# Where the pieces of a tile's second stage stand between the sums of the next tile: 1, 2, 2, 2, 2 in place of 2, 2, 2, 2, 1

## The chip, the core and the metric

The kernel runs on one core of a Trainium2 chip. TensorE (PE) multiplies, VectorE (DVE) and ScalarE (ACT) do the elementwise work, GpSimd (POOL) issues the gathers, SyncE (SP) the other transfers. The metric is the device time of one execution, in microseconds (us). The median of three runs before the change is 1955.56 us (1948.99 to 1957.19).

## What is computed

Two graph attention layers over 3327 nodes with 1024 features, each with a residual and a layer norm. The adjacency matrix is sparse (a few per mille of the entries, plus the diagonal). The change touches only the second layer, which has one head:

```python
h = input @ W
f1 = h @ a1
f2 = h @ a2
e = jax.nn.leaky_relu(f1 + f2.T, negative_slope=ALPHA)
scores = jnp.where(adj > 0, e, neg)
attention = jax.nn.softmax(scores, axis=1)
h_prime = attention @ h
return jax.nn.relu(h_prime)
...
x = _layernorm(x + _L1_gnn_ref(x, adj, L1_gnn_W, L1_gnn_a1, L1_gnn_a2), axis=-1)
```

Since attention @ (input @ W) is (attention @ input) @ W, the kernel first takes the weighted mean of the neighbours' input rows, and multiplies that mean by W afterwards.

## The kernel before

The nodes are 26 tiles of 128 targets. A first stage projects layer 0 and makes lists of neighbours; then layer 0 and layer 1 run one after the other through the same function, `pipeline`, and the change is in the call for layer 1 (L1083). A tile's edges are gathered in five steps: four blocks of four groups (32 targets each, 128 slots per group), and one "end" block for what did not fit.

For layer 1 (class `Target`) a tile t goes through these functions. `prepare` (L946) transposes a score column into the T bank on PE (L949), takes its exponential on ScalarE (L951) and makes one-hot marks on VectorE (L819, L823). `fetch` (L968) issues the gathers of one block on POOL (L803). `weights` (L974) makes a block's weights `es` by three operations on VectorE (L981, L982, L984). `sums` (L987) multiplies weights by gathered rows into three A banks (L993); for the four blocks it works in groups of 32 rows of the array, for the end block on all 128. `close` (L998) divides: the mean goes to `z` (L1001 to L1010, ScalarE and VectorE).

`finish` (L1015) is a generator of ten pieces. Pieces 1 and 2 (`transposed`, L176 and L179) transpose half of the mean each, four 128x128 blocks into one bank with the tag T, and ScalarE copies the bank to `xT`. Pieces 3 to 6 are the product of the mean with the first 512 columns of W (L1025), two matmuls to a piece, in a bank with the tag S; piece 6 ends with L1028, where VectorE takes the maximum with zero, adds the residual and so frees the bank. Pieces 7 to 10 do the same for the other 512 columns; piece 10 also queues `settle` (L1033), the layer norm (L192 to L199, with a square root on ScalarE, L195, that loads its own table) and the store.

In the profile one f32 matmul of L1025 or L993 leaves two records, so two pieces of the product are eight records.

Nothing is reordered by a scheduler here: the part runs under a manual schedule, and each engine executes in the order in which the program is written. That order comes from `pipeline`: at each step b of tile t it emits weights for the next step, the sums of this step, the gathers for the next tile, and then as many pieces of the waiting `finish` of the tile before as `behind[b]` says; `late` pieces are run at the beginning of a tile, ahead of its first sums. With late = 1 and a placeholder put in front at tile 1 (L1072), piece 10 of a `finish` is left to the beginning of the tile after. The eight PSUM banks are shared out by tag (L744): five A, one S, one T, and one E for `way`, where the weights are worked out. The core of the loop:

```python
for b in range(EB + 1):
    if b == 0 and t:
        tiles[t - 1].close()
        run(work, late)
    ...
    tg.sums(b)
    if t + 1 < NT:
        tiles[t + 1].fetch(b)
    run(work, behind[b])
    if t or b:
        run(ahead)
```

Of the kernel before, what the change touches and what calls it, by code (L numbers as in the profile page):

```python
# [26 lines left out]
def kernel(  # L27
# [715 lines left out]
    def sparse(own):  # L743
# [43 lines left out]
        def run(work, steps=1):  # L787

            while work and steps:
                try:  # L790
                    next(work[0])
                    steps -= 1
                except StopIteration:
                    work.popleft()
# [243 lines left out]
        def pipeline(kind, late, behind, get):  # L1038

            tiles = [kind(t) for t in range(NT)]
            work = deque()
            get(0)
            tiles[0].prepare()
            for b in range(EB + 1):
                tiles[0].fetch(b)
            tiles[0].weights(0)
            for t, tg in enumerate(tiles):  # L1050
                tg.begin()
# [4 lines that stand above are left out]
                    if b == 0 and t + 1 < NT:  # L1056
                        get(t + 1)
                    if b == 2 and t + 1 < NT:
                        tiles[t + 1].prepare()
                    if b == 0:  # L1060
                        tg.own()
                    if b < EB:
                        tg.weights(b + 1)
                    elif t + 1 < NT:
                        tiles[t + 1].weights(0)
# [6 lines that stand above are left out]
                if t == 0 and late:  # L1072
                    work.append(iter(range(1)))
                work.append(tg.finish())
            tiles[-1].close()
            run(work, late)
            run(ahead, -1)
            run(work, -1)
            run(ahead, -1)

        with tc.manual_schedule():
            pipeline(Layer0, 0, (1, 1, 1, 1, 1), get_edges)
            pipeline(Target, 1, (2, 2, 2, 2, 1), lambda t: None)  # L1083


    def by_pairs(own):
# [119 lines left out]
    with arm.Else():  # L1206
        with ExitStack() as own:
            sparse(own)
# [23 lines left out]
```

## Time and profile before

The profile is of one execution with a span of 1901.5 us. Rows below are sums over stretches of it (us of busy time, and what part of the stretch that is):

| stretch | what runs | PE | DVE | ACT | POOL | DMA GB/s |
|---|---|---|---|---|---|---|
| 0 to 450 us | projection, lists | 420.85 (94%) | 384.24 | 224.77 | 119.78 | 108 |
| 450 to 1200 us | layer 0 for the most part | 444.23 (59%) | 467.28 | 176.90 | 470.14 | 361 |
| 1210 to 1895 us | layer 1 | 653.32 (95%) | 292.51 | 144.70 | 432.51 | 356 |

In layer 1 the costliest groups are L1025 (383.3 us busy, 604 ns a record), L993 over gathered blocks (206.2 us, 464 ns a record, four of them side by side), and the gathers of L803 (415.7 us on POOL, 999 ns each). A row of the timeline has the start, the duration, the engine, the line, the operation, output and input, and how often; in brackets is the idle time of the engine ahead of it and what ended it. PEld is PE's weight load, which goes ahead of its matmul. A row of the list of waits has who waited for whom, the total in us, how often, and the longest.

### The profile page before, as it was taken

The page shows a single profiled execution, that of the slowest core. Times are in us where ns is not written, and L with a number is a line of the kernel's source. Part 1 is how long each engine was busy: PE and PEld are TensorE (multiplying, and loading weights), DVE is VectorE, ACT ScalarE, POOL GpSimd, SP SyncE. Part 2 cuts the span into 40 slices and gives each one's busy share as a digit, 9 for nine tenths or more (in the row PEclk, how much of TensorE's full clock was granted, in tenths as well). Part 3 has the DMA queues.
Part 4 walks back from the last instruction along what each step waited for, and adds up shares of the span by engine and source line. Part 5 has one row for each costly group of instructions (what it writes and reads, how often), then busy time and mean ns, then how long its engine had stood idle before and what let it go on. Part 6 is the DMA issues. An engine that isn't in the chain of part 4 may idle for free.

```text
span 1901.5 us, 38079 instructions
## 1 busy us (share of the span) xinstructions
PE 1518.5 (80%) x14663; PEld 902.4 (47%) x14663; DVE 1146.6 (60%) x3058; ACT 546.6 (29%) x1422; POOL 1030.2 (54%) x1391
## 2 busy tenths in 40 slices
PE   8799999999266555656556565399999999999997
PEld 5465556666255554545545454144444444444443
DVE  6699999986386665666666666244444444444442
ACT  5544455542022222222222222012222212222220
POOL 4322222220576666676676764677766667666650
PEclk9899999999678777787788877699999999999999
DMA  7656455411899999999999997899999999999980
GB/s 184 101 133 131 100 99 99 88 62 39 325 373 404 396 392 394 366 405 392 386 392 389 394 376 273 332 398 410 400 372 382 380 378 369 359 371 373 366 326 33
DMA packets 171068, 567.76 MB, mean 299 GB/s; under 512 B 27690, under 2 KB 34346, under 8 KB 170878
## 3 DMA queue, kind: packets, MB, share of 16 engines
q0 software_dynamic: 131056, 455.68, 67.6%
q1 hardware_dynamic: 39822, 109.56, 15.4%
q8 instruction: 118, 1.93, 0.4%
q14 instruction: 72, 0.59, 0.1%
HBM read 578.85 MB, written 42.97 MB: 327 GB/s over the span
## 4 chain that ended last, share of the span: by engine, by line
PE 52%; DMA 24%; DVE 12%; ACT 6%; issue 4%; POOL 2%; SPq 0%; DVEq 0%; ACTq 0%; POOLq 0%
DMA src<-h_d,idx 20%; PE mm L1025 20%; PE acc L993 12%; PE mm L479 12%; DVE e L870 3%; PE acc L898 3%; ACT junk L311 3%; PE tr L176 2%; POOL src L803 2%; DMA src<-y_d,idx 2%; DVE pr L931 1%; PE acc L882 1%; DMA wt<-in_L_gnn_W_dram 1%; ACT xT L179 1%; PE xp L411 1%
## 5 line engine op out<-in xcount | busy, mean ns | idle before, releaser
L803 POOL DMA_INDIRECT src<-h_d,idx x416 | 441.1, 1060 | 209.1 <-PE acc L898 58.0
L803 POOL DMA_INDIRECT src<-y_d,idx x416 | 415.7, 999 | 221.6 <-PE acc L993 96.3
L898 PE MATMUL acc<-src,e 128*32 128x128 f32 x6656 | 278.5, 337 | 253.6 <-DVE e L870 253.5
L479 PE MATMUL mm<-wt,xT 128*128 128x347 f32 (+1 forms) x1248 | 402.3, 469 | 3.3 <-DMA wt<-in_L_gnn_W_dram 2.9
L1025 PE MATMUL mm<-wt,xT 128*128 128x512 f32 x832 | 383.3, 604 | 0.8 <-DVE o L1028 0.8
L898 PEld LDWEIGHTS acc<-src,e 128*32 128x32 f32 x6656 | 234.8, 137 | 311.3 <-DVE e L870 284.3
L479 PEld LDWEIGHTS mm<-wt,xT 128*128 128x128 f32 x1248 | 228.3, 192 | 106.0 <-issue 4.2
L1025 PEld LDWEIGHTS mm<-wt,xT 128*128 128x128 f32 x832 | 152.2, 190 | 199.5 <-issue 179.1
L993 PE MATMUL acc<-src,es 128*32 128x342 f32 (+1 forms) x2496 | 206.2, 464 | 33.8 <-DVE es L984 31.0
L870 DVE TENSOR_TENSOR e<-oh,way 128x1024 f32<-128x1024 f32 x130 | 158.7, 1221 | 63.2 <-ACT w L868 62.8
L993 PEld LDWEIGHTS acc<-src,es 128*32 128x32 f32 x2496 | 71.6, 111 | 158.6 <-issue 112.9
L868 ACT ACTIVATE w<-way 128x32 f32<-128x32 f32 (+1 forms) x130 | 24.6, 189 | 407.7 <-DVE way L866 395.6
L1028 DVE SCALAR_TENSOR_TENSOR o<-mm,y 128x512 f32<-128x512 f32 x52 | 35.9, 691 | 166.2 <-PE mm L1025 166.2
L1007 ACT ACTIVATE z<-y,ri 128x342 f32<-128x342 f32 (+1 forms) x78 | 39.5, 570 | 313.9 <-DVE ri L1003 313.9
L865 DVE TENSOR_TENSOR way<-src,re 128x32 f32<-128x32 f32 x104 | 20.8, 200 | 175.1 <-DMA src<-h_d,idx 157.6
L179 ACT ACTIVATE xT<-tr 128x512 f32<-128x512 f32 x104 | 59.4, 596 | 151.0 <-PE tr L176 150.9
L981 DVE TENSOR_TENSOR way<-way,src 128x128 f32<-128x128 f32 x104 | 31.1, 299 | 90.0 <-ACT way L951 44.2
L850 ACT ACTIVATE own<-own,es 128x128 f32<-128x128 f32 x208 | 63.6, 388 | 57.4 <-DVE es L847 57.4
L311 ACT ACTIVATE junk<-ad 128x3328 uint8<-128x3328 uint8 x26 | 78.4, 3014 | 2.5 <-POOL ad L308 2.5
L882 PE MATMUL acc<-end,e 128*128 128x128 f32 x416 | 67.7, 328 | 13.3 <-DVE e L870 13.3
L296 POOL CAST mvs<-r 128x8 bf16<-128x8 f32 x26 | 6.0, 232 | 122.8 <-ACT r L295 122.8
L335 POOL TENSOR_TENSOR place_of<-cnt 128x1 f32<-128x1 f32 x26 | 4.9, 190 | 121.0 <-ACT cnt L328 101.5
(188 smaller groups left out, 1959.7 us busy)
## 6 DMA issues: line engine op xcount, KB each, us to landing
h_d<-ht SPq DMA_DIRECT2D x26, 520.0 KB
own<-h_d SPq DMA_DIRECT2D x26, 520.0 KB
y_d<-y SPq DMA_DIRECT2D x26, 514.0 KB
y<-y_d SPq DMA_DIRECT2D x26, 514.0 KB
x<-in_x_dram SPq DMA_DIRECT2D x25, 512.0 KB
y<-in_x_dram SPq DMA_DIRECT2D x25, 512.0 KB
out_dram<-o SPq DMA_DIRECT2D x25, 512.0 KB
ad<-in_adj_dram POOLq DMA_DIRECT2D x25, 415.9 KB
```

Source lines behind the costliest of these rows:

```text
L176: nc.tensor.transpose(tr[:, k, :], src[:, (4 * g + k) * P : (4 * g + k + 1) * P], ident)
L179: nc.scalar.activation(part, tr, AF.Copy)
L311: nc.scalar.activation(junk, ad, AF.Copy, accum_out=self.deg)
L479: nc.tensor.matmul(acc, xT[t][:, k, :], wt[:, k, CUTS0[c] : CUTS0[c + 1]], start=k == 0, stop=k == KT - 1)
L803: nc.gpsimd.indirect_dma_start(out=s[:, g, :w], out_offset=None, in_=table[:, :], in_offset=bass.IndirectOffsetOnAxis(ap=idx[:, t, b * NG ...
L850: nc.scalar.activation(hn, hn, AF.Copy, scale=es[:, n : n + 1])
L870: nc.vector.tensor_tensor(e, oh.unsqueeze(2).to_broadcast([P, ng, H, wide]), wp.unsqueeze(3).to_broadcast([P, ng, H, wide]), OP.mult,)
L882: nc.tensor.matmul(self.acc[h // 4][:, h % 4, :], e[:, 0, h, :], rowsof[:, 0, h, :], start=False, stop=h % 4 == 3,)
L898: nc.tensor.matmul(self.acc[h // 4][g * GT : (g + 1) * GT, h % 4, :], e[:, g, h, :], rowsof[:, g, h, :], start=first and h % 4 == 0, stop= ...
L993: nc.tensor.matmul(self.acc[c][to, :m], es[:, g, :], s[:, g, CUTS[c] : CUTS[c + 1]], start=b == 0, stop=b == EB,)
L1007: nc.scalar.activation(z[:, cut], self.res[:, cut], AF.Copy, scale=ri[:, 1:2])
L1025: nc.tensor.matmul(acc, xT[:, k, :], wt1[:, k, half], start=k == 0, stop=k == KT - 1)
```

## The change

One tuple: how many pieces of the waiting `finish` follow each of a tile's five sums in layer 1.

```diff
         with tc.manual_schedule():
             pipeline(Layer0, 0, (1, 1, 1, 1, 1), get_edges)
-            pipeline(Target, 1, (2, 2, 2, 2, 1), lambda t: None)
+            pipeline(Target, 1, (1, 2, 2, 2, 2), lambda t: None)
```

The number of pieces in a tile is the same. Both halves of transposes use the one T bank, so the second half can't begin before ScalarE has emptied the bank of the first. With the change the sums of the second step stand between the two halves. All later pieces move by one: the pieces after sums 0 to 4 were 1-2, 3-4, 5-6, 7-8 and 9, and are 1, 2-3, 4-5, 6-7 and 8-9. Piece 10 stays at the beginning of the tile after. On VectorE, L1028 of the first product moves behind the weights of the end block; on ScalarE, the square root of the layer norm comes to stand between the two copies to `xT`.

## Prediction

> **What bounds the kernel now.** I read the page first (engine shares, slices), then the busy time by windows inside layer 1, then the list of waits there, then the timeline of one tile, and last the timeline of the drain after the last tile, because a wait that the change creates already occurs there once. Layer 1 runs from about 1210 us to the end. The table by windows (columns: busy time and number of instructions of PE, PE's weight loads, DVE, ACT, POOL; clock; DMA share; GB/s) says who limits it; each window here is one tile, 26 us:
>
> ```profile
> 1485.00:1511.00 26.00, 25.31 (x146) 10.93 (x145) 11.45 (x34) 5.84 (x10) 17.44 (x18) 1.00 1.00 371
> 1511.00:1537.00 26.00, 25.31 (x146) 11.02 (x145) 11.75 (x36) 5.84 (x10) 17.31 (x18) 1.00 0.98 370
> ```
>
> PE is busy 25.31 of 26.00 us, at the full clock; DVE, ACT and POOL are far from full. So PE sets the pace, and the idle 0.69 us per tile is all that a reordering can take away directly. The waits between 1230 and 1880 us (total us, times, longest) name it:
>
> ```profile
> POOL src L803 <- PE acc L993: 96.0, 119, 3.7
> ...
> DVE way L981 <- DMA src<-y_d,idx: 17.6, 7, 4.2
> ...
> PE tr L176 <- ACT xT L179: 20.0, 26, 2.8
> ```
>
> The third line is the idle: the second group of transposes waits for ScalarE to empty the one T bank. Leaving out the longest (the drain), (20.0 - 2.8) / 25 = 0.69 us a tile. The gathers wait for PE to free source buffers (first line), and VectorE waited for gathered rows 7 times only, so DMA, though 98 to 100% busy by share, does not set the end here. In the timeline of one tile (start, duration) the wait looks like this:
>
> ```profile
> 1515.40 1.93 PE L993 MATMUL acc<-src,es 128*32 128x341 f32 x24
> ...
> 1517.26 0.43 PEld L176 LDWEIGHTS tr<-ident,z 128*128 128x128 f32 x4 [0.56 <-DVE way L982]
> ...
> 1517.96 0.60 ACT L179 ACTIVATE xT<-tr 128x512 f32<-128x512 f32 x1 [4.84 <-PE tr L176]
> 1518.61 0.42 PEld L176 LDWEIGHTS tr<-ident,z 128*128 128x128 f32 x4 [0.92 <-ACT xT L179]
> ...
> 1519.19 0.16 PEld L993 LDWEIGHTS acc<-src,es 128*32 128x32 f32 x8 [0.17 <-DVE sg L194]
> ...
> 1540.94 1.93 PE L993 MATMUL acc<-src,es 128*32 128x341 f32 x24
> ```
>
> From one tile's first sums to the next is 1540.94 - 1515.40 = 25.54 us. The first transposes hold PE from 1517.26 to 1518.61 (1.35 us, with the wait), the second from 1518.61 to 1519.19 (0.58 us, without one).
>
> The drain has the other wait. Here all ten pieces of the last tile stand in a row, so piece 7 follows piece 6 with nothing between, and both use the one S bank:
>
> ```profile
> 1876.15 0.42 PEld L176 LDWEIGHTS tr<-ident,z 128*128 128x128 f32 x4 [2.99 <-ACT xT L179]
> 1876.54 0.30 PEld L1025 LDWEIGHTS mm<-wt,xT 128*128 128x128 f32 x2
> ...
> 1884.36 0.19 PEld L1025 LDWEIGHTS mm<-wt,xT 128*128 128x128 f32 x1 [0.24 <-issue]
> 1886.16 0.30 PEld L1025 LDWEIGHTS mm<-wt,xT 128*128 128x128 f32 x2 [1.61 <-DVE o L1028]
> 1886.69 0.19 PEld L1025 LDWEIGHTS mm<-wt,xT 128*128 128x128 f32 x1 [0.24 <-issue]
> ```
>
> VectorE's own rows put that L1028 at 1885.41, for 0.69 us; the weight load follows 0.06 us after its end.
>
> [...] L1028 held VectorE 4.17 us in this tile while it waited for PE. [...] a weight load of L1025 after the 32-row sums comes 0.56 us after the last one, between products 0.24 us. [...] the trace's waits of 0.7 to 0.8 us are followed by loads at the usual 0.43 us, and only after the drain's 2.99 us do four come 0.85 us apart, so no clock is lost in the loop.
>
> **The change, part by part.** No instruction is added or removed, and the queues of POOL and SP stay the same. [...] It concerns the 25 finishes inside the loop; the last runs in the drain, which is the same.
>
> *The T wait goes.* Before, transposes cost 1.35 + 0.58 = 1.93 us a tile. After, half 1 is followed by sums 1, as half 2 was: 0.58 us. Half 2 then stands before a product in the same tiling mode: the drain shows 1876.54 - 1876.15 = 0.39 us for that. Gain 1.93 - 0.58 - 0.39 = 0.96 us; from below it is bounded by the idle 0.69 us. The copy of half 1 (0.60) lies beside sums 1 (1.87 us), that of half 2 beside piece 3 (four records at 0.43 = 1.72 us).
>
> *An S wait comes.* Pieces 6 and 7 now stand side by side, where sums 3 stood between them and hid L1028. Piece 7 waits until L1028 has emptied the bank. Price from the drain: from the last load before it to the third after its return 1886.69 - 1884.36 = 2.33 us, where three steps of 0.43 = 1.29 would do: 1.04 us. From below, PE's idle row there, 0.79; from above, the plain gap in loads, 1.80 - 0.43 = 1.37. I take 1.04, as the third load has both the restart and its catching up in it. Queued behind the waiting matmul are piece 7, sums 4, and then 8, 9, 10: all of PE. Nothing else fills it.
>
> *VectorE's order.* L1028 moves behind the three operations of weights(4) (3 x 0.30 us plus gaps, about 0.95). They need the end rows, gathered some 24 us before, and stood behind L1028 only by order; they now run before piece 6 ends, so L1028 is ready when PE is. Behind L1028 stand weights(0) of the next tile (0.95 us), whose sums come after sums 4 and three pieces, so over 7 us later. Cost nothing.
>
> *ScalarE's order.* The square root with its table load (1.28 + 0.20 us) now stands between the two xT copies. Counted from the sums 0 at 1515.40, with the durations of the same timeline: copy 1 ends at 3.2, the root's input is there at 3.7, the root ends at 4.7, or 5.2 if the table came late; half 2's transposes end near 5.0. Copy 2 then ends by 5.8, and L949, which needs the T bank, is due at 4.31 + 0.39 + 1.72 = 6.4. Hidden, with 0.6 us to spare.
>
> *Room elsewhere.* close() gets three pieces instead of two to hide under, but it ended 1.7 us early already: worth nothing. Sums 1 comes at 2.44 and its es was ready at 2.09 (1517.20 + 0.29): no wait, though close.
>
> Sum: (1.04 - 0.96) x 25 = +2.0 us, 1955.56 + 2.0 = 1957.6 us. With the bounds crossed: (0.79 - 0.96) x 25 = -4, (1.37 - 0.96) x 25 = +10, and (1.37 - 0.69) x 25 = +17.
>
> **The rivals.** *The exchange is about even* (above): 1957.6. *The T wait goes and the S wait is mostly hidden*: at the most 0.96 x 25 = 24, so 1932; half hidden, 1944. For it: L1028 might find PE with slack elsewhere. Against it: PE is 97% busy and its order is fixed, and the drain shows the S wait whole. *The S wait is larger*: at 1.37 and a gain of 0.69, 1973; if weights(4) held L1028 up by 0.95 us, (0.08 + 0.95) x 25 = +26, 1981. [...] Against it: VectorE idled over 4 us at L1028, which is more than weights(4) takes. *A wait at L949* behind root and table load: a microsecond a tile, +25, 1981; against it the 0.6 us to spare.
>
> **How the numbers follow.** Even exchange 0.70; T gain without its price 0.11; larger S wait 0.13; L949 0.06. Within 0.5% is 9.8 us, so faster 0.11, same 0.70, slower 0.19. The runs before spread 8 us of themselves. The range takes in the even exchange with its bounds and that spread, half of the faster rival and the start of the slower ones: 1945 to 1972.
>
> **What would show it.** Right: the wait of L176 on xT falls from 20 us to the drain's 2.8; a wait of L1025 on L1028 appears 25 more times at 0.8 us idle; the tile period is 25.6 us. Wrong: L1028 starting later than 0.1 us after piece 6 ends, a wait of L949 on xT, of sums 1 on es, or a new wait for gathered rows; or a period of 24.7, if the S wait were hidden.

## The result, and the profile after

| | median us | lowest to highest | executions |
|---|---|---|---|
| before | 1956.38 | 1948.99 to 1958.43 | 4 |
| after | 2022.80 | 2019.75 to 2023.61 | 4 |

The ratio is 1.0326, with a 95% interval of 1.0301 to 1.0352: slower by 66 us. The prediction was 1957.6, in a range that ended at 1972. It was wrong, and no rival reached this time either.

The profile after spans 2017.7 us. The list of waits of PE in the middle of layer 1, 1310 to 1930 us, has the same columns as the one shown of before (total us, times, longest). A line that ends in "issue" is an idle time for which this trace holds no releasing event; the timeline below shows what such a line stands for.

```profile
PE tr L949 <- issue: 20.8, 18, 1.9
PE mm L1025 <- issue: 20.6, 13, 2.2
PE mm L1025 <- DVE o L1028: 20.6, 9, 6.5
PE tr L949 <- ACT xT L179: 4.2, 3, 1.9
```

The wait of L176 on `xT` is gone, as foretold. The wait of piece 7 on L1028 has come, but with 41.2 us (20.6 + 20.6, in 22 places) it is 1.87 us on the mean, not 0.79. And L949, which was to be hidden with 0.6 us to spare, waits 21 times, 25.0 us in all.

One tile of the timeline after (start, duration, engine, line, operation, output and input, how often, idle time ahead and what ended it):

```profile
1632.29 0.66 PE L176 MATMUL tr<-ident,z 128*128 128x128 f32 x4
1632.98 0.60 ACT L179 ACTIVATE xT<-tr 128x512 f32<-128x512 f32 x1 [6.56 <-PE tr L176]
...
1634.74 0.66 PE L176 MATMUL tr<-ident,z 128*128 128x128 f32 x4
1634.89 0.20 ACT L195 ACTIVATE sg<-sg 128x1 f32<-128x1 f32 x1
...
1635.23 1.88 PE L1025 MATMUL mm<-wt,xT 128*128 128x512 f32 x4
...
1637.64 0.60 ACT L179 ACTIVATE xT<-tr 128x512 f32<-128x512 f32 x1 [2.55 <-PE mm L1025]
...
1638.30 0.32 PE L949 MATMUL tr<-ident,sd 128*128 128x128 f32 x1 [1.18 <-issue]
...
1645.90 1.98 PE L1025 MATMUL mm<-wt,xT 128*128 128x512 f32 x4
...
1648.69 0.69 DVE L1028 SCALAR_TENSOR_TENSOR o<-mm,y 128x512 f32<-128x512 f32 x1 [6.76 <-PE mm L1025]
...
1649.44 1.99 PE L1025 MATMUL mm<-wt,xT 128*128 128x512 f32 x4 [1.55 <-DVE o L1028]
```

Copy 1 starts 0.03 us after half 1 ends (1632.29 + 0.66 = 1632.95). Half 2 ends at 1635.40, ScalarE is free since 1635.09 (the root, L195), and nothing but PE is left to wait for: yet copy 2 starts at 1637.64, 2.24 us late. The trace has an event of PE's semaphore at 1637.62, just before that start, so by this trace it is the signal that comes late, and not ScalarE that answers it late. L949 needs the bank that copy 2 empties, and so comes 1.18 us after piece 3. The same at piece 6: it ends at 1647.88, VectorE has been idle for 6.76 us, and L1028 starts at 1648.69, 0.81 us late (the event before it is at 1648.67); piece 7 then idles 1.55 us.

The table by windows has the same tile (columns as before: busy time and number of PE, PE's loads, DVE, ACT, POOL; clock; DMA share; GB/s):

```profile
1632.29:1660.09 27.80, 25.07 (x147) 10.56 (x143) 11.37 (x34) 5.84 (x10) 16.94 (x17) 1.00 0.92 341
```

The tile takes 27.80 us at full clock; 25.62 was predicted. Three tiles in the middle of this profile take 31.6 to 34.5 us, and some at the beginning of layer 1 take longer than steady ones too. In one of the three L1028 is so late that piece 7 waits 6.51 us, and its four records then take 3.78 us instead of 1.98 (the second row, again from the timeline after). In another tile a wait of 2.06 us is followed by four records in 2.83 us (the first row):

```profile
1469.14 2.83 PE L1025 MATMUL mm<-wt,xT 128*128 128x512 f32 x4 [2.06 <-issue]
1529.89 3.78 PE L1025 MATMUL mm<-wt,xT 128*128 128x512 f32 x4 [6.51 <-DVE o L1028]
```

The granted clock is 0.50 from 1470.2 to 1473.5 us, after the wait of 2.06 us, and 0.50 from 1530 to 1535, after the one of 6.51. Another wait of 2.10 us in the same profile (it ends at 1297.89) was followed by four records in the usual 1.98, so the length of a wait doesn't tell it by itself. So such a wait can be paid for twice.

### The profile page after: what moved, and what is told of

It reads as the page before. It is cut to its first block, busy times and chain, and to the rows that moved or that the text cites. A ratio compares the mean times of both kernels' runs of the same rounds, so it can differ in the third digit from the quotient of the medians.

```text
span 2017.7 us, 38080 instructions
## 1 busy us (share of the span) xinstructions
PE 1673.8 (83%) x14663; PEld 936.4 (46%) x14663; DVE 1142.0 (57%) x3058; ACT 546.1 (27%) x1422; POOL 1029.3 (51%) x1391
## 4 chain that ended last, share of the span: by engine, by line
PE 71%; issue 12%; DVE 6%; ACT 5%; DMA 3%; another core or an unknown queue 2%; POOL 1%; SPq 0%; POOLq 0%; DVEq 0%; ACTq 0%
PE mm L1025 19%; PE acc L898 17%; PE acc L993 12%; PE mm L479 11%; PE acc L882 5%; PE acc L890 3%; ACT junk L311 3%; PE tr L176 2%; DMA src<-h_d,idx 1%; DMA wt<-in_L_gnn_W_dram 1%; PE den L907 1%; PE xp L411 1%; DVE top L274 1%; DMA src<-y_d,idx 1%
## 5 line engine op out<-in xcount | busy, mean ns | idle before, releaser
L898 PE MATMUL acc<-src,e 128*32 128x128 f32 x6656 | 376.8, 298 | 165.2 <-issue 134.5
L1025 PE MATMUL mm<-wt,xT 128*128 128x512 f32 x832 | 392.4, 610 | 46.4 <-DVE o L1028 23.7
L898 PEld LDWEIGHTS acc<-src,e 128*32 128x32 f32 x6656 | 231.0, 118 | 322.5 <-issue 283.7
L1025 PEld LDWEIGHTS mm<-wt,xT 128*128 128x128 f32 x832 | 151.6, 192 | 241.3 <-issue 202.7
L993 PE MATMUL acc<-src,es 128*32 128x342 f32 (+1 forms) x2496 | 216.2, 466 | 41.9 <-DVE es L984 24.3
L1028 DVE SCALAR_TENSOR_TENSOR o<-mm,y 128x512 f32<-128x512 f32 x52 | 36.0, 692 | 288.9 <-PE mm L1025 266.1
L882 PE MATMUL acc<-end,e 128*128 128x128 f32 x416 | 96.1, 424 | 1.6 <-DVE e L870 1.6
L882 PEld LDWEIGHTS acc<-end,e 128*128 128x128 f32 x416 | 88.8, 325 | 2.3 <-DVE e L870 1.7
```

Of the source, the lines that this page charges most:

```text
L882: nc.tensor.matmul(self.acc[h // 4][:, h % 4, :], e[:, 0, h, :], rowsof[:, 0, h, :], start=False, stop=h % 4 == 3,)
L898: nc.tensor.matmul(self.acc[h // 4][g * GT : (g + 1) * GT, h % 4, :], e[:, g, h, :], rowsof[:, g, h, :], start=first and h % 4 == 0, stop= ...
L993: nc.tensor.matmul(self.acc[c][to, :m], es[:, g, :], s[:, g, CUTS[c] : CUTS[c + 1]], start=b == 0, stop=b == EB,)
L1025: nc.tensor.matmul(acc, xT[:, k, :], wt1[:, k, half], start=k == 0, stop=k == KT - 1)
```

## Experiments: each half of the change alone, on a chip where it works as priced

The profile of before from which all prices were taken spans 1901.5 us, 54 us less than the times beside it. The result of each experiment names the chip that it ran on, by a number; for the first comparison, of before and after, no chip is on record. The first three kernels ran on chip 11, where before takes 1901.89 us (median of 7).

The order before, unchanged, and the two halves of the change: in the first the T wait goes and no S wait comes, in the second the T wait stays and the S wait comes.

```diff
# c0_before_again: no edit
# e1_t_alone
-            pipeline(Target, 1, (2, 2, 2, 2, 1), lambda t: None)
+            pipeline(Target, 1, (1, 3, 2, 2, 1), lambda t: None)
# e2_s_alone
-            pipeline(Target, 1, (2, 2, 2, 2, 1), lambda t: None)
+            pipeline(Target, 1, (2, 1, 2, 2, 2), lambda t: None)
```

> The kernel before, unchanged, profiled once more: the profile that the prediction was read from spans 1901.5 us while the timed runs of the same kernel have a median of 1956. If that profile is typical, this one again shows 25.5 us from L949 to L949 in layer 1 and the first L993 at about 1210 us. If it was a quick execution and the kernel usually runs slower, the first L993 comes near 1238 us as in the kernel after, and the tiles of layer 1 take 26 us or more.

> Pieces 1, 3, 2, 2, 1: sums 1 stand between the two halves of transposes, but pieces 5-6 and 7-8 keep sums 3 between them, so the T wait is taken out and no S wait is made. Theory A (each wait has its own price, and the S wait or what hangs on it is dearer than thought): 25 x 0.96 = 24 us faster than before. Theory B (the layer norm's square root, now between the two copies on ScalarE, holds up the second copy and with it L949 and the tile): as slow as the kernel after in part, 1.1 us a tile, +28 us less the 24 gained, so about the same as before. Theory C (the slower time has nothing to do with the order of the pieces, layer 0 being slower as well): about +60 us as in the kernel after.

> Pieces 2, 1, 2, 2, 2: both halves stay together and the T wait stays, while pieces 6 and 7 stand side by side as in the kernel after. Theory A: all of the loss is here, +66 + 24 = about +90 us. By the price of the prediction +26 us. Theory B: +26 us, the rest of the loss lies with the second copy, which is not moved here. Theory C: about +60 us.

| chip 11 | us | ratio to before, 95% | tile, L949 to L949 |
|---|---|---|---|
| before again | 1901.80 | one execution | 25.54 |
| T wait gone alone | 1879.82 | 0.9890 (0.9864 to 0.9915) | 24.59 |
| S wait alone | 1928.42 | 1.0148 (1.0129 to 1.0167) | 26.59 |

The first half brings 0.95 us a tile where 0.96 was worked out; the second costs 1.05 where 1.04 was. The waits of PE over 1290 to 1860 us say the same; first the T wait gone (the one line left is the drain's), then the S wait alone:

```profile
PE tr L176 <- ACT xT L179: 2.8, 1, 2.8
```

```profile
PE mm L1025 <- DVE o L1028: 16.5, 21, 0.8
PE tr L176 <- ACT xT L179: 14.4, 21, 0.7
```

So both prices were right, and on this chip the two halves add up to 26.53 - 22.07 = 4.46 us; the whole change didn't run there. Here, copy 2 and L1028 start 0.04 us after the end of the PE instruction they wait for, in every tile of all three profiles.

## Experiments: the same kernels on a chip where PE's completions come late

The changed kernel again, then before, after and the two halves together. Both groups ran on chip 5. The edits are those above; nothing else is changed.

> The kernel after, unchanged. The two halves of the change gave -22 and +26.5 us by themselves, in a session where the kernel before runs at 1902 us and not at 1956. Theory A (the two exchanges add up wherever the kernel runs as it does in that session, and what made the first comparison +66 us is something of that session in which PE's semaphores reach ScalarE and VectorE 0.8 to 2.2 us late): before at 1902, and this +2 to +5 us, tiles of 25.6 us, copies and L1028 0.04 us after PE's end. Theory B (the two edits disturb each other when both are made, since the second copy and L949 get close): before at 1902, this +40 to +66 us, with tiles of 27.8 us. If the session is like the first, with before at 1956: +66 us again, and the trace with its tiles of 27.8 us.

> The kernel before, on the same chip as the next three, whichever it is. On the chip of the halves it ran at 1902 us, on those of the two runs of the kernel after at 1956 and 1978. Theory A (a slower chip lets PE's finished work reach ScalarE and VectorE late, whatever the order of the pieces): on a slow chip this too shows copies to xT and L1028 starting 0.8 to 3 us after PE's end, and tiles over 25.5 us. Theory B (only the kernel after has the late starts, since only in it do half 2 and piece 6 stand right before a stalled PE, and the slow chip merely adds DMA time): 0.04 us everywhere, tiles of 25.5 us, the time added in layer 0.

> The kernel after. On a slow chip both theories have the tiles of 27.8 to 28 us again. On a fast one, theory A has +2 to +5 us over before, theory B +40 us or more, the two halves disturbing each other.

> Pieces 1, 3, 2, 2, 1. On a slow chip, theory A: the second copy starts 2 us late here as well, so that the 24 us gained are lost in part or whole; theory B: 20 to 24 us faster than before also here, the second copy at 0.04 us. On a fast one both have it 22 us faster.

> Pieces 2, 1, 2, 2, 2. On a slow chip, theory A: L1028 of piece 6 starts 0.8 us or more late, +26 and another 20 us; theory B: +26 us, L1028 at 0.04 us. On a fast one +26 us.

"Late" below is the start of copy 2, or of L1028 of piece 6, less the end of the last PE row it waits for, both from the timeline; the median of 20 tiles from the middle of layer 1. The end of a PE row is modelled, so "late" holds whatever lies between the modelled end and the consumer's start. On chip 11 that was 0.04 us.

| run, chip | us | ratio to before, 95% | tile, median | copy 2 late | L1028 late |
|---|---|---|---|---|---|
| after, first comparison (chip not on record) | 2022.80 | 1.0326 (1.0301 to 1.0352) | 27.79 | 2.22 | 0.80 |
| after again, 5 | 2075.03 | 1.0505 (1.0470 to 1.0540) | 28.74 | 3.04 | 0.27 |
| before, 5 | 1981.77 | 0.9988 (0.9969 to 1.0008) | 25.63 | 0.04 | 0.04 |
| after, 5 | 2083.83 | 1.0496 (1.0460 to 1.0533) | 29.51 | 3.06 | 1.19 |
| T wait gone alone, 5 | 1995.77 | 1.0074 (1.0057 to 1.0091) | 26.54 | 3.28 | 0.04 |
| S wait alone, 5 | 2048.12 | 1.0317 (1.0281 to 1.0352) | 28.06 | 0.04 | 0.90 |

Before takes 1977.74 us in the first of these groups and 1980.24 in the second. The half that gave 22 us on chip 11 costs 15 here; the half that cost 26 costs 68; the whole costs 97 to 104. The waits of PE at 1340 to 1930 us, with the T wait gone alone:

```profile
PE acc L993 <- DVE es L984: 15.1, 11, 1.7
PE tr L949 <- issue: 9.3, 11, 2.8
PE acc L993 <- DVE way L982: 5.1, 6, 1.4
```

None of these lines exists on chip 11. L949 waits behind a late copy 2; sums 1 wait for weights that stand on VectorE behind a late L1028 of piece 10.

One comparison goes against what a queue on paper says. The kernel with the S wait alone differs from the changed one only by the T wait, put back at the old place. On chip 11 the T wait costs 0.95 us a tile. On chip 5 the kernel that has it is 2083.83 - 2048.12 = 36 us *faster* (two executions of each). In it copy 2 is never late. There PE waits between the halves, and no stretch of sums runs between them; which of the two matters isn't separated.

Other parts of the kernel show it too. The share of PE by slices in layer 0 (tenths, 40 slices), which the change doesn't touch, and the group of L898, its sums: first the page of after in the first comparison, then that of the same kernel on chip 13 (next but one section).

```profile
PE   8799999995677777777777882888997998889997
...
L898 PE MATMUL acc<-src,e 128*32 128x128 f32 x6656 | 376.8, 298 | 165.2 <-issue 134.5
```

```profile
PE   8799999999366655656555665499999999999997
...
L898 PE MATMUL acc<-src,e 128*32 128x128 f32 x6656 | 272.5, 332 | 247.8 <-DVE e L870 247.7
```

Same code, same number of instructions, but in slices 12 to 21 PE is called busy for 7 tenths instead of 5 or 6, and 134.5 us of idle time in front of L898 have no releaser that the trace shows.

## Experiments: moving the wait, and fewer records, on chip 5

Four kernels together, on chip 5 again; before takes 1957.93 us this time (43 executions, 1950.45 to 1976.28), so a chip's time isn't fixed either. In the first, L949 is issued one step later, far from copy 2. The second is the T wait gone alone, with L949 moved and with the weights of block 1 ahead of the late L1028. The third and fourth are the order after and before with 3 matmuls over all 128 rows in place of 12 over 32 in each block: a quarter of the records in the same time. These two leave out the edges of three of the four groups of each block, though the gathers still bring their rows.

```diff
# f1_after_l949_late: the changed kernel, and
-                    if b == 2 and t + 1 < NT:
+                    if b == (3 if kind is Target else 2) and t + 1 < NT:
# f2_t_alone_both_moved: (1, 3, 2, 2, 1), the edit above, and
-                        tiles[t - 1].close()
+                        tiles[t - 1].close(), kind is Target and tg.weights(1)
...
-                        tg.weights(b + 1)
+                        b == 0 < t and kind is Target or tg.weights(b + 1)
# f3_after_few_records: the changed kernel, and
-                    for g in range(NG if b < EB else 1):
-                        to = slice(g * GT, (g + 1) * GT) if b < EB else slice(0, P)
+                    for g in range(1):
+                        to = slice(0, P)
                         nc.tensor.matmul(
-                            self.acc[c][to, :m], es[:, g, :], s[:, g, CUTS[c] : CUTS[c + 1]],
+                            self.acc[c][to, :m], es.rearrange("p g t -> p (g t)"), s[:, g, CUTS[c] : CUTS[c + 1]],
# f4_before_few_records: the kernel before, and the last edit
```

> The order 1, 2, 2, 2, 2 with prepare one step later (b == 3 in layer 1), so that L949 takes the T bank some seven us after copy 2, not right behind it. Theory (completions of PE reach ScalarE late on chips such as chip 5, so that copy 2 is late and L949 waits for it): on chip 5 the idle of PE at L949 (23.3 + 9.3 = 32.6 us over some 22 tiles in the run of the order 1, 2, 2, 2, 2 there) goes, and copy 2 stays late by some 3 us, which then costs nothing until piece 3: about 2083 - 35 = 2048 against 1980 before. Rival (copy 2 and L949 are late as everything is, and the wait only moves to the next operation): over 2075 as without it. On a chip such as chip 11, where completions come in 0.04 us, both theories expect no gain: 1904 against 1902.

> The order 1, 3, 2, 2, 1 (T wait gone, no S wait) with two things moved that waited behind late completions on chip 5: prepare one step later (L949 away from copy 2), and the weights of block 1 on VectorE ahead of the L1028 of piece 10. Theory: on chip 5 the waits of L949 (8.8 + 3.6 + 0.8) and of L993 on es (11.8, 5.1) go, some 30 us of 1996: about 1960, under before's 1980; on chip 11 the 1880 of the order 1, 3, 2, 2, 1 stays. Rival (the order itself costs the chip something, whatever waits where): 1990 or more on chip 5.

> The order 1, 2, 2, 2, 2, with each block's sums made by 3 matmuls over all 128 rows, as the end block's are, in place of 12 over 32 rows: 6 records in place of 24 in the same 1.9 us. Leaves out the edges of three of the four groups of every block of layer 1 (the gathers still bring them). Theory (a dense stretch of PE instructions piles up completions, which drain afterwards): on chip 5 copy 2 starts 0.04 us after its transposes instead of 3 us, L1028 of piece 6 0.04 us after its product, L949 doesn't wait, tiles come at about 25 us, and layer 1 is within 10 us of that of the order 2, 2, 2, 2, 1 with the same sums. Rival (completions are slow on chip 5 however many there are): copy 2 late by 2 to 3 us and the time some 90 us above that of the order 2, 2, 2, 2, 1 with the same sums. On chip 11 both: 0.04 us, and the two orders within 5 us.

> The control to the few records: the order 2, 2, 2, 2, 1 with each block's sums made by 3 matmuls over all 128 rows in place of 12 over 32 (the same edges left out). On chip 5 L1028 of piece 10, late by some 1.5 us in half of the tiles with the many records: by the theory of piled-up completions it starts at 0.04 us; by the rival it stays late. Both: the time is some 25 to 40 us under before[...].

| chip 5 | us | ratio to before, 95% | copy 2 late | L1028 late |
|---|---|---|---|---|
| after, L949 moved | 2067.25 | 1.0564 (1.0511 to 1.0617) | 2.94 | 2.63 |
| T wait gone, both moved | 1954.55 | 0.9976 (0.9956 to 0.9997) | 3.37 | 0.56 |
| after, few records | 1961.20 | 1.0006 (0.9985 to 1.0027) | 0.04 | 0.04 |
| before, few records | 1957.57 | 0.9985 (0.9962 to 1.0009) | 0.04 | 0.04 |

**L949 moved: my theory fell, its rival stood.** 35 us were to come back; the kernel lies 109 us above before. A tile of its timeline:

```profile
1563.39 0.66 PE L176 MATMUL tr<-ident,z 128*128 128x128 f32 x4
...
1566.28 0.60 ACT L179 ACTIVATE xT<-tr 128x512 f32<-128x512 f32 x1 [2.53 <-PE mm L1025]
...
1571.09 0.27 PE L949 MATMUL tr<-ident,sd 128*128 128x128 f32 x1
...
1573.56 1.98 PE L1025 MATMUL mm<-wt,xT 128*128 128x512 f32 x4
...
1578.73 0.69 DVE L1028 SCALAR_TENSOR_TENSOR o<-mm,y 128x512 f32<-128x512 f32 x1 [3.03 <-remote]
1579.48 2.93 PE L1025 MATMUL mm<-wt,xT 128*128 128x512 f32 x3 [3.94 <-issue]
```

L949 (1571.09) doesn't wait any more, but L1028 starts 3.2 us after piece 6 ends (1575.54), where it was 0.81 us late in the tile shown of after, and piece 7 idles 3.94 us. The lateness wasn't L949's; it is carried on until PE has to wait for something. PE's waits at L949 and L1025 come to 84.4 us in the order after (1340 to 2000 us, same chip) and to 70.4 us here (1320 to 1980), now all at L1025, and one long wait is paid for twice here too: after the 3.94 us three records take 2.93 us, where four took 1.98 before it.

**T wait gone, both moved:** both waits left the list, and the time is 3.4 us under before, where the same order without the moves lay 15 us above before in its own group. Some 20 us under before were expected: the direction is right, the size is not. It is the only kernel without the T wait, and with all its work, that did not lose on chip 5; it has not run on another chip.

**Few records: the theory held where it speaks of the order, and missed elsewhere.** With 6 records in place of 24 per block, copy 2 is late in none of the 20 tiles, and the order after costs 1961.20 - 1957.57 = 3.6 us more than the order before, where it cost 97 to 104 with the full number. The trace of the order after is of an execution of 1983.64 us; three of its 16 executions lie above 1980 us, and this is one of them. A tile of the timeline of the order after with few records:

```profile
1561.58 0.60 PE L176 MATMUL tr<-ident,z 128*128 128x128 f32 x4
...
1562.22 0.60 ACT L179 ACTIVATE xT<-tr 128x512 f32<-128x512 f32 x1 [0.23 <-PE tr L176]
...
1563.74 0.27 PE L949 MATMUL tr<-ident,sd 128*128 128x128 f32 x1
```

So the loss hangs on how many instructions the sums issue (or on their 32-row form or the work left out, which were changed with the number), not on the order alone. But a gain of 25 to 40 us against before, for which no measured price had been worked out, was expected of the control and isn't there, L1028 of piece 6 was still 1.8 to 4.1 us late in 5 of the 20 tiles of the order after, and L1028 of piece 10 was late by 2.6 us (median) and L1001 by up to 6 us in the order before. "Fewer instructions, nothing late" would be too simple.

## Experiments: the change on other quick chips, a wait put back, and no gathers

Two things were left open: whether PE's waits are what lets late completions catch up (a transpose and a one-column copy are added ahead of half 2, so that PE waits there again), and whether the gathers' traffic makes them late (layer 1's gathers are left out from the third tile on). These ran on chip 13 (before: 1899.12, 47 executions), and two of them once more on chip 3 (1905.40, 24 executions). In all six traces copy 2 and L1028 start 0.04 us after PE, so neither question was answered. What they do give is the change itself on such a chip.

```diff
# g0_after_third: the changed kernel
# g1_after_and_a_stall, h1_after_and_a_stall: the changed kernel, and
-                yield from ph.transposed(xT, z, (0, 1))
+                for n, _ in enumerate(ph.transposed(xT, z, (0, 1))): yield; n or nc.scalar.activation(sbuf("jj", [P, 1], 2), nc.tensor.transpose(d := bank("T", [P, P], "tr"), z[:, :P], ident) and d[:, :1], AF.Copy)
# g2_after_no_gathers, h2_after_no_gathers: the changed kernel, and (g3_before_no_gathers: the kernel before, and)
-                self.src[b] = gather(y_d, HW, self.t, b)
+                self.src[b] = gather(y_d, HW, self.t, b) if self.t < 2 else srcs[(self.t * EB + b) % NS] if b < EB else ends[self.t % 2]
```

> The order 1, 2, 2, 2, 2 again, beside the three others. On chip 5 some 95 to 110 us above before, with copy 2 late by 2 to 3 us and L1028 of piece 6 by about 1; on a chip such as chip 11 the prediction's +2, with both at 0.04 us.

> The order 1, 2, 2, 2, 2 with one transpose of 128x128 into the T bank and a ScalarE copy of one column of it put ahead of half 2, in every tile: half 2 then waits about 0.7 to 1 us for that copy, as it waited for copy 1 in the order 2, 2, 2, 2, 1. Theory (a wait of PE lets the late completions catch up; the T wait did that before): on chip 5 copy 2 starts within 0.1 to 0.7 us of its transposes, L949 no longer waits (1.2 to 2 us a tile), and the kernel with more work in it is 10 to 40 us faster than the order 1, 2, 2, 2, 2 without it. Rival (the lateness has nothing to do with PE's waits): the added operation costs 25 x 1 us or more, 25 to 75 us slower than without it. On a chip such as chip 11 both: about 25 us slower than without it.

> The order 1, 2, 2, 2, 2; leaves out layer 1's gathers from the third tile on (the sums read the rows that the first tiles gathered), everything else is there. Theory (the gathers' traffic is what makes completions late): on chip 5 copy 2 and L1028 of piece 6 start 0.04 us after PE, tiles come at some 25.6 us, and the time is within 10 us of the order 2, 2, 2, 2, 1 without gathers. Rival (PE's own density of instructions does it alone): copy 2 late by 2 to 3 us and 80 to 110 us above the order 2, 2, 2, 2, 1 without gathers.

> The control: the order 2, 2, 2, 2, 1 without layer 1's gathers from the third tile on (left out as in the run above). If traffic makes completions late, L1001, late by some 2 us on chip 5 in most tiles, starts at 0.04 us, and the time falls by the tiles above 25.5 us, some 20 to 40 us under before; if not, L1001 stays late and the time is at most 15 us under before.

> The order 1, 2, 2, 2, 2 with an added transpose and a ScalarE copy of one column ahead of half 2 in every tile, which makes PE wait there. On a chip such as 13: 19 to 20 us above before. On chip 5, theory (a wait of PE lets late completions catch up): copy 2 within 0.7 us of its transposes, no wait at L949, 60 to 90 us above before, so 10 to 40 under the 97 to 103 that the order costs there without the added wait. Rival (PE's waits have nothing to do with it): 120 to 170 us above before.

> The order 1, 2, 2, 2, 2; leaves out layer 1's gathers from the third tile on. On a chip such as 13: 4 us above before, tiles of 25.6 us. On chip 5, theory (the gathers' traffic makes completions late): copy 2 and L1028 of piece 6 0.04 us after PE in nearly all tiles, tiles of some 25.6 us, at most 15 us above before. Rival (PE's density of instructions alone makes them late): copy 2 late by 2 to 3 us, 80 to 110 us above before.

| run, chip | us | ratio to before, 95% | tile |
|---|---|---|---|
| after, 13 | 1902.54 | 1.0019 (1.0012 to 1.0026) | 25.64 |
| after and a wait, 13 | 1918.68 | 1.0103 (1.0086 to 1.0120) | 26.23 |
| after, no gathers, 13 | 1903.10 | 1.0022 (1.0015 to 1.0029) | 25.64 |
| before, no gathers, 13 | 1896.93 | 0.9987 (0.9978 to 0.9996) | 25.54 |
| after and a wait, 3 | 1923.66 | 1.0096 (1.0061 to 1.0131) | 26.23 |
| after, no gathers, 3 | 1909.51 | 1.0022 (1.0012 to 1.0032) | 25.64 |

On chip 13 the change costs 1902.54 - 1899.12 = 3.4 us, by the interval 2.3 to 4.9; +2.0 was predicted. Its timeline holds the sums of the prediction one by one:

```profile
1515.70 0.66 PE L176 MATMUL tr<-ident,z 128*128 128x128 f32 x4
1515.85 0.20 ACT L195 ACTIVATE sg<-sg 128x1 f32<-128x1 f32 x1
...
1516.20 1.88 PE L1025 MATMUL mm<-wt,xT 128*128 128x512 f32 x4
1516.40 0.60 ACT L179 ACTIVATE xT<-tr 128x512 f32<-128x512 f32 x1 [0.34 <-PE tr L176]
...
1517.91 0.27 PE L949 MATMUL tr<-ident,sd 128*128 128x128 f32 x1
...
1525.47 1.98 PE L1025 MATMUL mm<-wt,xT 128*128 128x512 f32 x4
...
1527.50 0.69 DVE L1028 SCALAR_TENSOR_TENSOR o<-mm,y 128x512 f32<-128x512 f32 x1 [6.81 <-PE mm L1025]
...
1528.24 1.99 PE L1025 MATMUL mm<-wt,xT 128*128 128x512 f32 x4 [0.78 <-DVE o L1028]
```

Copy 2 ends at 1517.00, and L949 begins at 1517.91 without a wait. Piece 7 idles 0.78 us. Set beside the tile of after shown first, the two steps are the whole loss: from piece 3 to L949 it is 1517.91 - 1516.20 = 1.71 us here and 1638.30 - 1635.23 = 3.07 there, from piece 6 to piece 7 it is 2.77 here and 3.54 there. Together 1.36 + 0.77 = 2.13 us, of the 27.80 - 25.64 = 2.16 us between the tiles.

Without gathers the time falls by 2.2 us for the order before and not at all for the order after, so on this chip DMA, busy as it is (a share of 0.97 in the tile of the changed kernel shown above), sets next to nothing, as the prediction held. That does not say whether its traffic makes completions late on chip 5.

## Why the prediction was wrong, point by point

- **The T wait's price (0.96 us a tile): right.** 0.95 on chip 11, done alone.
- **The S wait's price (1.04): right on a chip without late completions.** 1.05 on chip 11, done alone, and 0.78 us of PE idle on chip 13, where 0.79 was foretold. In the first comparison L1028 started 0.81 us late, and the idle was 1.55 us in the tile shown, 1.87 on the mean. So this term was too small there, by 0.77 us in the tile shown. The upper bound, 1.37, was no bound: it came from the same profile, in which nothing is late.
- **"Hidden, with 0.6 us to spare" (copy 2 and L949): this is the step that failed most.** It put the wait of L949 at nothing because it counted copy 2 from the end of half 2's transposes, with no time between PE's end and ScalarE's start. On chip 13 that holds, with 0.9 us to spare. In the first comparison copy 2 was 2.24 us late (median 2.22), which eats the slack and leaves 1.18 us of idle in the tile shown, 1.36 in its length. The S wait's price rests on the same assumption for L1028. The rival "L949 waits" had this wait, but by another cause: it blamed the root with its table load, which was over at 1635.09.
- **The order on VectorE (weights ahead of L1028): right.** VectorE idles 6.76 us before L1028 in the tile after; it was ready and waiting.
- **`close`, sums 1, the gathers: right.** None of them shows in the list of waits after, but for one wait of 0.3 us before sums (the list has no more lines than the four shown and that one), and on chip 13 leaving the gathers out is worth about 2 us.
- **The sum:** predicted 0.08 us a tile, measured 0.10 on quick chips (25.54 to 25.64, the one on chip 11, the other on chip 13), and some 2.2 in a steady tile of the first comparison. Layer 1 of the changed kernel, from its first sums to the end, takes 779.6 us there and 696.0 on chip 13, 83.6 more. Steady tiles would make 25 x 2.16 = 54 us of that; the longer ones add the rest. Of the whole, 24 us are PE's busy time (675.8 us from 1240 to 2015 us there, 651.5 from 1205 to 1896 on chip 13, at mean granted clocks of 0.96 and 0.99) and the rest is idle. How the measured 66 us divide can't be said, as no trace shows the order before in the executions that it is compared with.

The first mistake lay ahead of all steps. The profile's span was 1901.5 us, the times 1949 to 1957, and I took every duration and every slack from the profile without asking where the other 54 us were. No trace of those longer executions is on record, but the runs on chip 5 are of the same kind: there, with before, layer 1 begins at 1259.9 us instead of 1208.6 on chip 11, L1028 and L1001 are late in part of the tiles, and layer 1 takes 718.2 us instead of 691.5, 27 more. The order after takes 818.4 us there instead of 696.0 on chip 13, 122 more. That the prediction's sum comes out within 2 us on chip 13 is no luck, since each of its two prices was measured alone; but it is a sum for chips of that kind, set on a base time of the other. The prediction had a line for it ("L1028 starting later than 0.1 us after piece 6 ends"), but gave such cases 0.19 together, and none of their sizes was worked out from a late completion.

**What stays open** is why completions are late there. Shown is that they are late on chip 5 and not on chips 3, 11 and 13, in the kernels that ran there; that the change's loss appears only with them; and that it nearly goes (97 to 104 us to 3.6) when the sums have a quarter of the instructions. Not shown is the cause. All runs on chip 5 lie within about half an hour, those on chip 11 before it and those on chips 13 and 3 after it, so the chip and the time aren't separated. In the first trace of after, recorded events of PE's semaphore come in groups some 0.7 us apart where L1028 waits (1646.47, 1647.19 to 1647.28, 1647.94 to 1647.98 and 1648.67), and in layer 0 PE pauses about that often: where two records of L898 start over 0.2 us apart, the next such place follows after 0.76 us in the median, most often after four records. On chip 13, and in the profile of before, such places come only every 64 records. My estimate from these times is that in the first trace of after the events get through only in a group every 0.7 us or so; what would hold them up was not shown, as no run separates one cause from another. No run compares executions with and without the profiler, so it isn't shown either that the loss exists when nothing is recorded. One candidate, the gathers' traffic, met no chip on which it could be tried. Whether a wait of PE lets late completions catch up is only argued, from the T wait that made a kernel 36 us faster.

**A version that beats both** depends on the chip. (1, 3, 2, 2, 1) takes 1879.82 us on chip 11, 22 us under before, and loses 15 on chip 5. With L949 and the weights of block 1 moved it is 3.4 us under before on chip 5.

## What to carry to other kernels

Compare a profile's span with the times before taking a single duration from it: a gap of 3%, as here, may mean that other executions or other chips have waits that this profile doesn't show, and slack of under a microsecond or two is then no slack (0.6 us were counted on here, and copy 2 came 2.2 to 3.4 us late). A wait in a tight loop may be hiding lateness elsewhere (on chip 5 the kernel with the T wait put back was 36 us faster), so before it is taken away, ask of every consumer behind it how late its producer's completion may come, and put work between a producer and the engine that must wait for it (with L949 and the weights of block 1 moved, the order without the T wait went from 15 us above before to 3.4 under it on chip 5; with L949 alone moved, the whole change still lay 109 us above). Measure a change of order on more than one chip.

## What the runs showed that was not expected

- The same kernel before takes 1899 to 1905 us on chips 3, 11 and 13, and 1958 to 1980 us on chip 5, at different times; the first comparison had 1956.
- The delay from the modelled end of a PE instruction to the start of the ScalarE or VectorE instruction that waits for it is 0.04 us on the quick chips, and in the order after has medians of 2.2 to 3.1 us at copy 2 on chip 5 and in the first comparison.
- Taking one wait that cost 0.95 us out of a tile, with nothing put in its place, made the kernel 22 us faster on one chip and 15 us slower on another.
- Traces of the chips with late completions hold fewer events: for the order before, 3333 events of PE's semaphore beside 3728 instructions that raise it on chip 5, 3687 on chip 11; in the first comparison's trace of after, 3346 beside 3752. There, a releaser named "issue" or "remote" may stand for an event that isn't in the trace.
- After waits of about 2 us PE's granted clock was halved in some tiles (2.06 us, then 2.83 us for four records) and not in others (2.10 us, then 1.98).
